# One loop for query mixing and the residual stage beside the edge products of a graph layer

## The chip, the cores and the metric

The kernel runs on one core of a Trainium2 chip. Times are device microseconds of that core for one execution. The time before is 3857.89 us, the median of 9 runs (3855.28 to 3866.76). The engines are named as the profile names them: PE (TensorE), DVE (VectorE), ACT (ScalarE), POOL (GpSimd) and SP (SyncE); SP only issues transfers here, and ACT and POOL issue some beside their own work.

## What is computed

A graph layer on 10,000 nodes with 512 features and 160,000 edges, sorted by destination, all in float32:

```python
xn = _layernorm(x, axis=-1)
x = x + _L0_gnn_ref(xn, W, bias, edge_weight, src, dst) + _L0_mix_ref(xn[None], w_qkv, w_out, gamma)[0]
x = x + _L0_ffn_ref(_layernorm(x)[None], router_w, W1, b1, W2, b2)[0]

# gnn: the kernel sums the rows of xn first and multiplies by W afterwards
h = X @ W;  msgs = h[edge_src] * edge_weight[:, None]
agg = segment_sum(msgs, edge_dst);  return relu(agg + bias)
# mix: linear attention, 8 heads of 64
q = softmax(q, axis=-1) * scale;  k = softmax(k, axis=-2)
context = einsum('bhnd,bhne->bhde', k, v)
out = einsum('bhde,bhnd->bhne', context, q);  out = gamma_layer_norm(out @ w_out.T, gamma)
# ffn: 6 experts, weights chosen from the mean row, gelu between W1 and W2
```

## The kernel before

The nodes are cut into 20 chunks of 512 rows (128 partitions by `SUB` = 4 rows; the last chunk has 272 rows). The stages follow each other, with the edge sums laid between the products of the first three:

- **Keys and queries.** `normal_rows` writes the normalised rows to DRAM (`xn_d`). For each chunk the loop computes the exponentials of keys and queries (`pk`, `pq`), adds keys times rows to `G`, and writes the transposed softmax of the queries to DRAM (`qT_d`).
- **Edges.** Edges are taken in groups of six tiles of 128. Line 327 gathers one tile of source rows by an indirect transfer that POOL issues (`msg`); lines 333 to 339 build on DVE a selection matrix `sel` (which of 64 destination rows a tile's edge belongs to, times its weight); line 345 multiplies them on PE (`pm`, two groups of three into the two halves of a PSUM bank); line 348 copies the sums out on ACT and line 349 writes them to `part_d` in DRAM. There are 209 groups, the last with two tiles. A destination whose edges cross a border between windows is put together by `carry`, for 128 windows (64 groups) at a time.
- **Mixing matrix.** After the keys, `edges_to(AT_HAND[0][1] // GROUP + 7)` runs edge groups with no other products between them until 135 are done; a conditional (`general_path`, line 456, not taken here) follows; then `mix` is computed (line 655 to 669), with one edge group between its steps.
- **Query loop.** For each chunk: load `qT` and the rows `xt` of x, multiply by `mix` (`po`, line 186), copy to `ot` on ACT, normalise (`row_stats`, lines 693 and 695, which also adds x), write to `y_d`.
- **Residual loop.** For each chunk: gather the edge sums by row (`at`, line 814, four indirect transfers), transpose them to `aT` (line 178, copied out by ACT and DVE in turn), multiply by the layer's weights (`pg`, line 186), add the bias (`gt`, line 836), apply relu and add `yt`, which is `y_d` loaded again (line 841), write `x1_d`, take the row statistics, normalise (`gt`, line 161), write `xn2_d`, and add the rows to `xsum` on POOL (line 849). `far_enough` runs edges up to the window that the chunk's rows may need (`AT_HAND`: chunks below 7 need windows below 256, chunks below 16 need 384, the rest all).
- **Experts.** 20 chunks of products with PE nearly always busy (line 1004). Their weights (`w1_sb`, `w2_sb`) are loaded when the edges are done and their memory is free (lines 741 and 742, from SP), and `w1_sum` is formed from them on DVE.

What sets the order: PE runs in the order of the program (`manual_schedule`). The other engines' streams are ordered by the framework's scheduler and then run in order. `work(us)` spreads the edges: each call counts the time of the products just issued (0.83 us per product of 128 by 512), and one group is issued for every `PACE` us counted. `msg` has 24 buffers, four groups. `row_stats` computes the inverse root on POOL (line 157, a power of -0.5), in one stream with the gathers. The products and transposes of the stages share six PSUM buffers, and the edge sums have two more.

Of the kernel before, what the change touches and what calls it, by code (L numbers as in the profile page):

```python
# [16 lines left out]
P = 128  # L17
SQ = 32
# [10 lines left out]
PACE = 5.4  # L29

AT_HAND = [(7, 256), (16, 384)]
# [8 lines left out]
def gps_layer_kernel(  # L40
# [41 lines left out]
    def tokens(t, c):  # L82
# [24 lines left out]
    from_last = const.tile([P, P], F32, name="from_last")  # L107
    nc.gpsimd.memset(from_last, 1.0)
    nc.gpsimd.affine_select(from_last, from_last, pattern=[[0, P]], compare_op=ALU.is_ge, fill=0.0,
                            base=1 - P, channel_multiplier=1)  # L110
# [21 lines left out]
    y_d = [dram.tile([r, SUB, D], F32, name=f"y_d{c}") for c, (_, r) in enumerate(chunks)]  # L132
# [8 lines left out]
    ZERO_ROW = NQ * P  # L141
    far_rows = -(-(N + P) // (8 * P)) * 8 * P
    assert far_rows <= AT_HAND[0][1] * WIN and NW < NQ * GROUP
    assert all(n <= NCH and w % P == 0 and w < NW for n, w in AT_HAND)
    part_d = dram.tile([ZERO_ROW + P, D], F32, name="part_d")
    by_window = part_d.rearrange("(w q) d -> w q d", q=WIN)
    nc.scalar.dma_start(part_d[ZERO_ROW : ZERO_ROW + P, :], zero)

    def row_stats(t, r, mv):

        st = small.tile([P, SUB, nc.vector.BN_STATS_DIM], F32, name="st")
        for s in range(SUB):
            nc.vector.bn_stats(st[:r, s, :], t[:r, s, :])  # L153
            nc.vector.bn_aggr(mv[:r, s, :], st[:r, s, :])
        ve = small.tile([P, SUB], F32, name="ve")
        nc.vector.tensor_scalar_add(ve[:r], mv[:r, :, 1], EPS)
        nc.gpsimd.tensor_tensor(mv[:r, :, 1], ve[:r], half_neg[:r], ALU.pow)
# [15 lines left out]
    def transposed(o, t, r, psum, tag):  # L173

        for kb in range(KB):
# [4 lines left out]
            (nc.scalar.copy if kb % 2 else nc.vector.tensor_copy)(  # L180
# [12 lines left out]

    edge_ctx = ctx.enter_context(ExitStack())
    query_ctx = ctx.enter_context(ExitStack())
    with ExitStack() as ph:
        mixing = edge_ctx.enter_context(tc.tile_pool(name="b_w", bufs=1))
        wq = mixing.tile([P, KB, D], F32, name="wq")
        G = mixing.tile([P, KB, D], F32, name="G")
# [16 lines left out]
        def normal_rows(n):  # L216

            for c in range(len(normal), min(len(normal) + n, NCH)):
# [4 lines left out]
                row_stats(xt, r, mv)  # L223
# [29 lines left out]
        def place_edges():  # L253
# [32 lines left out]
            nc.vector.memset(jump[:, 0:1], 1.0)  # L286
# [30 lines left out]
        def edges(i):  # L317
# [12 lines left out]
            sel = ew.tile([P, GROUP * BATCH, WIN], F32, name="sel")  # L330
# [8 lines left out]
            nc.vector.tensor_copy(sel[:, :n, 0:1], on_w[:, t0 : t0 + n, None])  # L339
            pm = psum_e.tile([P, D], F32, name="pm")  # L340
# [8 lines left out]
            nc.scalar.dma_start(part_d[i * P : (i + 1) * P, :], part)  # L349
# [3 lines left out]
        NJ = -(-NW // P)  # L353
        nexts = ep.tile([P, NJ], F32, name="nexts")
        held = {}
# [30 lines left out]
        def next_nodes():  # L386
            pn = psum.tile([P, NJ], F32, name="pnext", tag="ps")
            for b in range(NJ):
                r = min(P, NW - b * P)
                nc.tensor.transpose(pn[:r, b : b + 1], bases[0:1, b * P + 1 : b * P + 1 + r], ident[0:1, 0:1])  # L390
            nc.vector.tensor_copy(nexts[:, : NJ - 1], pn[:, : NJ - 1])
            r = NW - (NJ - 1) * P
            nc.vector.tensor_copy(nexts[:r, NJ - 1 :], pn[:r, NJ - 1 :])

        def carry_loads(b):
            r = min(P, NW - b * P)
            on = ew.tile([P, D], F32, name="on", bufs=1)
            nc.scalar.dma_start(on[:r], by_window[b * P : b * P + r, 0, :])
            own = ew.tile([P, D], F32, name="own", bufs=1)
            nc.scalar.dma_start(own[:r], by_window[b * P + 1 : b * P + 1 + r, 1, :])  # L400
            held["loads"] = on, own

        def carry(b):
            r = min(P, NW - b * P)
            on, own = held.pop("loads")
            to = bases[:, b * P + 1 : b * P + 1 + r]
# [3 lines left out]
            if b:  # L410
                same0 = ew.tile([P, P], F32, name="same0", bufs=1)
                nc.vector.scalar_tensor_tensor(same0[:, :r], to, bases[:, b * P : b * P + 1], from_last[:, :r],
                                               op0=ALU.is_equal, op1=ALU.mult)
            pt = psum.tile([P, D], F32, name="pcarry", tag="ps")
            nc.tensor.matmul(pt[:r], same[:r, :r], on[:r], start=True, stop=not b)
            if b:
                nc.tensor.matmul(pt[:r], same0[:, :r], held["total"], start=False, stop=True)
            if b < NJ - 1:
                held["total"] = ew.tile([P, D], F32, name="total", bufs=2)
                nc.scalar.copy(held["total"], pt)  # L420
            nc.vector.tensor_tensor(own[:r], own[:r], pt[:r], ALU.add)
            nc.scalar.dma_start(by_window[b * P + 1 : b * P + 1 + r, 1, :], own[:r])
# [4 lines left out]
        def edges_to(stop):  # L427
            while done[0] < stop:
                i = done[0]
                edges(i)  # L430
                done[0] += 1
                b, past_end = divmod(i, P // GROUP)
                if b and past_end == 1:
                    carry_loads(b - 1)
                if b and past_end == 6:
                    carry(b - 1)
# [197 lines left out]

        edges_to(AT_HAND[0][1] // GROUP + 7)
# [37 lines left out]
        dp = mean_ctx.enter_context(tc.tile_pool(name="d_w", bufs=1, side="right", reuse_waits="tile"))  # L673
        wg = dp.tile([P, KB, D], F32, name="wg")
        nc.sync.dma_start(wg, gnn_w.rearrange("(k p) d -> p k d", p=P))
        xsum = dp.tile([P, D], F32, name="xsum")
        nc.vector.memset(xsum, 0.0)
        io = query_ctx.enter_context(tc.tile_pool(name="c_io", bufs=2, side="right", reuse_waits="tile"))
        for c, (_, r) in enumerate(chunks):
            qT = io.tile([P, KB, SUB * P], F32, name="qT")  # L680
            nc.sync.dma_start(qT[:, :, : SUB * r], qT_d[c])
            xt = io.tile([P, SUB, D], F32, name="xt")
            nc.sync.dma_start(xt[:r], tokens(x, c))
            ot = io.tile([P, SUB, D], F32, name="ot")
            for s in range(SUB):
                po = psum.tile([P, D], F32, name="po", tag="ps")
                times(po, qT, s, r, mix)
                work(KB * PRODUCT)
                nc.scalar.copy(ot[:r, s, :], po[:r, :])
            mv = small.tile([P, SUB, 2], F32, name="mv")  # L690
# [6 lines left out]
            nc.sync.dma_start(y_d[c], ot[:r])  # L697
# [3 lines left out]

    PAIRS = NBASE // 2
    PLAIN = range(2 * PAIRS, NBASE)
    HALF = 2 * P
    KH, DH = KB // 2, D // 2
    assert KB % 2 == 0 and NF - NBASE <= PAIRS and all(fsz[f] == P for f in range(NBASE))
    def sums_of(o, a11, a12, a21, a22):

        nc.vector.tensor_tensor(o[0], a21, a22, ALU.add)
        nc.vector.tensor_tensor(o[2], a11, a21, ALU.subtract)
        nc.vector.tensor_tensor(o[1], o[0], a11, ALU.subtract)
        nc.vector.tensor_tensor(o[3], a12, o[1], ALU.subtract)

    def sums_for(o, b11, b12, b21, b22):

        nc.vector.tensor_tensor(o[0], b12, b11, ALU.subtract)
        nc.vector.tensor_tensor(o[2], b22, b12, ALU.subtract)
        nc.vector.tensor_tensor(o[1], b22, o[0], ALU.subtract)  # L720
        nc.vector.tensor_tensor(o[3], b21, o[1], ALU.subtract)

    io_f = {}
    held_w = {}

    def experts_weights():
        wp = held_w["pool"] = ctx.enter_context(tc.tile_pool(name="f_w", bufs=1, reuse_waits="tile"))
        w1_sb = held_w["w1"] = wp.tile([P, KB, NBASE * P], F32, name="w1_sb")
        w2_sb = held_w["w2"] = wp.tile([P, NBASE, D], F32, name="w2_sb")
        held_w["w1_sum"] = wp.tile([P, 4, KH, PAIRS * P], F32, name="w1_sum")  # L730
        b1_sb = held_w["b1"] = wp.tile([P, NF], F32, name="b1_sb")
# [480 lines left out]
```

## Time and profile before

| What | us |
|---|---|
| median of 9 runs | 3857.89 |
| the profiled execution's own time | 3863.09 |
| its span | 3861.4 |
| keys and queries, to the last product | 0 to 1303.45 |
| edges alone | 1303.45 to 1405.54 |
| no PE work, up to the mixing matrix | 1405.54 to 1425.60 |
| mixing matrix | 1425.60 to 1465.10 |
| wait for the first queries | 1465.10 to 1477.95 |
| query loop | 1477.95 to 1849.60 |
| residual loop | 1849.60 to 2480.42 |
| experts | 2480.42 to 3861.4 |

The borders are starts and ends of PE instructions in the timeline. A product of 128 by 512 in float32 is two instructions on PE and takes about 0.88 us of its time; an edge group is twelve instructions. The 40 slices of the page are 96.5 us each. "Idle before" a line is the time in which its engine did nothing just before it, and after the arrow stands what ended that time; "issue" means that nothing the profile shows ended it, which for in-order streams is often the instruction ahead in the queue.

### The profile page before, as it was taken

The numbers are of one execution on the slowest core, as the hardware profiler recorded it, in microseconds if no ns is written. First come the engines' busy times: TensorE is split into PE (matmuls) and PEld (weight loads), VectorE is DVE, ScalarE is ACT, GpSimd is POOL, SyncE is SP. The second block draws the span as 40 slices with busy tenths as digits, with TensorE's granted clock in tenths as the row PEclk, the third lists the DMA queues.
The fourth block names the chain that finished last, engine by engine and source line by source line (L and its number), as shares of the span: only waits on it lengthen the run. The fifth ranks groups of instructions, "written<-read, shape, count | busy, mean of one in ns | idle before, by whom it ended". The sixth has DMA issues, their size and how long they took to land.

```text
span 3861.4 us, 35880 instructions
## 1 busy us (share of the span) xinstructions
PE 3538.1 (92%) x12896; PEld 2028.2 (53%) x12896; DVE 1767.1 (46%) x3659; ACT 649.0 (17%) x1233; POOL 1586.7 (41%) x1565
## 2 busy tenths in 40 slices
PE   6999999999999748999675797899999999999998
PEld 3434343434343213333231243478888888888887
DVE  7843333333333214555352375764554545455452
ACT  4311111111111101111100000021111212111121
POOL 7656666666666662477687675400000000000000
PEclk9999999999999878999888898999999999999999
DMA  9667777777777766799787678612222112222210
GB/s 368 243 197 242 233 226 249 228 254 224 251 220 227 223 204 231 289 343 341 233 287 246 204 259 252 222 44 55 77 55 77 53 49 74 55 77 55 74 37 35
DMA packets 227061, 706.06 MB, mean 183 GB/s; under 512 B 36151, under 2 KB 76087, under 8 KB 195024
## 3 DMA queue, kind: packets, MB, share of 16 engines
q0 software_dynamic: 106720, 348.25, 29.1%
q1 hardware_dynamic: 72656, 194.76, 15.6%
q10 hardware_dynamic: 47492, 160.60, 10.8%
q8 instruction: 106, 1.74, 0.2%
q14 instruction: 87, 0.71, 0.1%
HBM read 504.22 MB, written 199.26 MB: 182 GB/s over the span
## 4 chain that ended last, share of the span: by engine, by line
PE 47%; DVE 5%; issue 5%; DMA 4%; POOL 1%; ACTq 0%; ACT 0%; SPq 0%; DVEq 0%; POOLq 0%
PE px L1004 13%; PE pz L1004 9%; PE py L1004 9%; PE po L186 7%; PE pm L345 3%; PE pg L186 3%; PE ph L1004 2%; DVE gt L161 1%; DMA msg<-xn_d,src_sb 1%; DMA z_d<-xt 1%; POOL msg L327 1%; DVE st L153 1%; DVE yt L841 1%; DMA xt<-x_d 1%; DVE gt L836 1%
## 5 line engine op out<-in xcount | busy, mean ns | idle before, releaser
L327 POOL DMA_INDIRECT msg<-xn_d,src_sb x1250 | 1230.6, 984 | 625.8 <-issue 303.8
L345 PE MATMUL pm<-msg,sel 128*64 128x512 f32 x2502 | 630.4, 629 | 105.0 <-issue 72.5
L345 PEld LDWEIGHTS pm<-msg,sel 128*64 128x64 f32 x2502 | 171.0, 142 | 539.0 <-issue 460.2
L186 PE MATMUL pg<-wg,aT 128*128 128x512 f32 (+1 forms) x640 | 297.6, 621 | 50.8 <-DVE gt L836 43.9
L186 PE MATMUL po<-G,qT 128*128 128x512 f32 (+1 forms) x640 | 285.8, 600 | 15.8 <-DMA qT<-qT_d 12.8
L613 PE MATMUL pc<-xn,ek 128*128 128x512 f32 (+1 forms) x640 | 287.8, 597 | 1.5 <-DVE G L616 1.1
L186 PE MATMUL pk<-wk,xnT 128*128 128x512 f32 (+1 forms) x640 | 287.9, 600 | 1.4 <-issue 1.1
L186 PE MATMUL pq<-wq,xnT 128*128 128x512 f32 (+1 forms) x640 | 287.1, 599 | 0.0
L333 DVE TENSOR_TENSOR sel<-iota_w,place 128x378 f32<-128x378 f32 (+1 forms) x209 | 123.4, 590 | 351.4 <-remote 165.7
L348 ACT COPY part<-pm 128x512 f32<-128x512 f32 x209 | 122.5, 586 | 854.0 <-PE pm L345 450.8
L186 PEld LDWEIGHTS pg<-wg,aT 128*128 128x128 f32 (+1 forms) x640 | 122.9, 197 | 213.3 <-issue 151.1
L1004 PE MATMUL px<-xnT,w_sb 128*128 128x256 f32 (+1 forms) x800 | 204.6, 378 | 15.9 <-DVE u L1039 15.9
L186 PEld LDWEIGHTS po<-G,qT 128*128 128x128 f32 (+1 forms) x640 | 118.1, 188 | 182.9 <-issue 182.9
L186 PEld LDWEIGHTS pk<-wk,xnT 128*128 128x128 f32 (+1 forms) x640 | 117.0, 188 | 168.6 <-issue 164.0
L186 PEld LDWEIGHTS pq<-wq,xnT 128*128 128x128 f32 (+1 forms) x640 | 116.6, 187 | 168.0 <-issue 166.3
L613 PEld LDWEIGHTS pc<-xn,ek 128*128 128x128 f32 (+1 forms) x640 | 116.9, 190 | 144.0 <-issue 137.5
L1004 PE MATMUL px<-w_sb,hh 128*128 128x256 f32 (+1 forms) x800 | 186.3, 380 | 0.0
L1004 PE MATMUL py<-xs,w_sum 128*128 128x256 f32 (+1 forms) x800 | 185.0, 374 | 0.0
L1004 PE MATMUL py<-w_sum,hh 128*128 128x256 f32 (+1 forms) x800 | 179.2, 379 | 0.0
L1004 PEld LDWEIGHTS px<-xnT,w_sb 128*128 128x128 f32 x800 | 150.5, 192 | 39.0 <-DVE u L1039 19.2
L1004 PEld LDWEIGHTS px<-w_sb,hh 128*128 128x128 f32 (+1 forms) x800 | 150.6, 188 | 22.9
L1004 PEld LDWEIGHTS py<-w_sum,hh 128*128 128x128 f32 (+1 forms) x800 | 150.0, 188 | 22.7
(254 smaller groups left out, 4433.4 us busy)
## 6 DMA issues: line engine op xcount, KB each, us to landing
part_d<-part ACTq DMA_DIRECT2D x209, 256.0 KB
msg<-xn_d,src_sb POOLq DMA_INDIRECT x1250
xn<-in_x SPq DMA_DIRECT2D x19, 1024.0 KB
xn_d<-xn ACTq DMA_DIRECT2D x19, 1024.0 KB
qT_d<-qT ACTq DMA_DIRECT2D x19, 1024.0 KB
qT<-qT_d SPq DMA_DIRECT2D x19, 1024.0 KB
xt<-in_x SPq DMA_DIRECT2D x19, 1024.0 KB
y_d<-ot SPq DMA_DIRECT2D x19, 1024.0 KB
```

The costliest lines, as they stand in the source:

```text
L153: nc.vector.bn_stats(st[:r, s, :], t[:r, s, :])
L161: (nc.vector if s < SUB - pool else nc.gpsimd).tensor_scalar(o[:r, s, :], t[:r, s, :], mv[:r, s, 0:1], mv[:r, s, 1:2], op0=ALU.subtract, o ...
L186: nc.tensor.matmul(po[:r, :], t[:, kb, s * r : (s + 1) * r], w[:, kb, :], start=kb == 0, stop=kb == KB - 1)
L327: nc.gpsimd.indirect_dma_start(out=m[k], out_offset=None, in_=xn_d, in_offset=bass.IndirectOffsetOnAxis(ap=src_sb[:, t0 + k : t0 + k + 1], ...
L333: nc.vector.tensor_tensor(sel[:, :n, 1:], iota_w[:, None, :].to_broadcast([P, n, WIN - 1]), place[:, t0 : t0 + n, None].to_broadcast([P, n ...
L345: nc.tensor.matmul(pm[h * WIN : (h + 1) * WIN, :], sel[:, k, :], m[k] if k < n else m[0], start=j == 0, stop=j == BATCH - 1 or k >= n - 1, ...
L348: nc.scalar.copy(part, pm)
L613: nc.tensor.matmul(pc, ek[:r, s, cb * P : (cb + 1) * P], xn[:r, s, :], start=s == 0, stop=s == SUB - 1)
L836: nc.vector.tensor_tensor(gt[:r, s, :], po[:r, :], bias_b[:r], ALU.add)
L841: nc.vector.scalar_tensor_tensor(yt[:r], gt[:r], 0.0, yt[:r], op0=ALU.max, op1=ALU.add)
L1004: nc.tensor.matmul(o, lhs[j], rhs[j], start=start and j == 0, stop=stop and j == n - 1, skip_group_check=True)
```

## The change

The query loop and the residual loop become one loop over the chunks. A chunk's mixed rows stay in SBUF (`ot`); `y_d` with its write and its read is gone. The rows gathered for the branch (`at`) are transposed before the last of the four query products, all four copied by ACT, and the layer's products `pg` follow the query products of the same chunk. `pg` plus bias goes into the chunk's `xt`, which the mixing part has finished with; later the normalised rows go there too. `qT` and `aT` have one buffer each.

- The stretch of edges alone after the keys is taken out; `PACE` goes from 5.4 to 5.0; the window limits become finer (`AT_HAND`, `CARRIES`: carries after 128, 256, 320, 384 windows and the rest), and `part_d` is moved behind a region of its own for the untaken path.
- Gathers and selections of a group are issued two groups ahead of its products (`edges_in`, `AHEAD`), with four buffers of `sel`.
- `row_stats` after the keys takes the root on ACT and a reciprocal and one correction step on DVE; the normalisation at the start keeps POOL's power.
- `xsum` is added on DVE; `x1_d` and `xn2_d` are written from SP, not ACT; the experts' weights are loaded from POOL's queue, not SP's.
- `w1_sum` and the first chunk for the experts are formed inside the loop (`c == NCH - 3`, `c == NCH - 2`).

In the order of instructions that the changed program has, 132 groups lie before the end of the keys (122 before), 5 in the mixing matrix as before, and the other 72 in the new loop, between the second chunk and the middle of the sixteenth.

```diff
-PACE = 5.4
-AT_HAND = [(7, 256), (16, 384)]
+PACE = 5.0
+AT_HAND = [(5, 128), (11, 256), (14, 320), (17, 384)]
+CARRIES = [0, 128, 256, 320, 384]
+AHEAD = 2
+LEAD = 5
...
-        nc.gpsimd.tensor_tensor(mv[:r, :, 1], ve[:r], half_neg[:r], ALU.pow)
+        if on_pool:
+            nc.gpsimd.tensor_tensor(mv[:r, :, 1], ve[:r], half_neg[:r], ALU.pow)
+            return
+        root = small.tile([P, SUB], F32, name="root")
+        nc.scalar.activation(root[:r], ve[:r], AF.Sqrt)
+        nc.vector.reciprocal(root[:r], root[:r])
+        near = small.tile([P, SUB], F32, name="near")
+        nc.vector.tensor_tensor(near[:r], root[:r], root[:r], ALU.mult)
+        nc.vector.scalar_tensor_tensor(near[:r], near[:r], -0.5, ve[:r], op0=ALU.mult, op1=ALU.mult)
+        nc.vector.scalar_tensor_tensor(mv[:r, :, 1], near[:r], 1.5, root[:r], op0=ALU.add, op1=ALU.mult)
...
-                nc.sync.dma_start(w1_sb[g * SQ : (g + 1) * SQ, j, :], features(w1)[j, g, :, : NBASE * P])
-        nc.sync.dma_start(w2_sb, w2[: NBASE * P, :].rearrange("(f p) d -> p f d", p=P))
+                nc.gpsimd.dma_start(w1_sb[g * SQ : (g + 1) * SQ, j, :], features(w1)[j, g, :, : NBASE * P])
+        nc.gpsimd.dma_start(w2_sb, w2[: NBASE * P, :].rearrange("(f p) d -> p f d", p=P))
...
-            sel = ew.tile([P, GROUP * BATCH, WIN], F32, name="sel")
+            sel = ew.tile([P, GROUP * BATCH, WIN], F32, name="sel", bufs=AHEAD + 2)
...
+            return n, m, sel
+        def edges_summed(i, n, m, sel):
             pm = psum_e.tile([P, D], F32, name="pm")
...
         def edges_to(stop):
             while done[0] < stop:
                 i = done[0]
-                edges(i)
+                while len(held["edges"]) <= AHEAD and i + len(held["edges"]) < NQ:
+                    held["edges"].append(edges_in(i + len(held["edges"])))
+                edges_summed(i, *held["edges"].pop(0))
                 done[0] += 1
...
-        edges_to(AT_HAND[0][1] // GROUP + 7)
         keys_ctx.close()
...
+        def queries_in(c):
+            qT = io.tile([P, KB, SUB * P], F32, name="qT", bufs=1)
+            nc.sync.dma_start(qT[:, :, : SUB * chunks[c][1]], qT_d[c])
+            return qT
...
         for c, (_, r) in enumerate(chunks):
-            qT = io.tile([P, KB, SUB * P], F32, name="qT")
-            nc.sync.dma_start(qT[:, :, : SUB * r], qT_d[c])
-            xt = io.tile([P, SUB, D], F32, name="xt")
-            nc.sync.dma_start(xt[:r], tokens(x, c))
+            xt = xt_next
             ot = io.tile([P, SUB, D], F32, name="ot")
             for s in range(SUB):
+                if s == SUB - 1:
+                    aT = io.tile([P, KB, SUB * P], F32, name="aT", bufs=1)
+                    transposed(aT, at, r, psum, "ps", by_act=range(KB))
+                    if c + 1 < NCH:
+                        at = gathered(c + 1)
                 po = psum.tile([P, D], F32, name="po", tag="ps")
                 times(po, qT, s, r, mix)
-                work(KB * PRODUCT)
+                put_out(KB * PRODUCT)
                 nc.scalar.copy(ot[:r, s, :], po[:r, :])
+            if c + 1 < NCH:
+                qT = queries_in(c + 1)
+                xt_next = rows_again(c + 1)
             mv = small.tile([P, SUB, 2], F32, name="mv")
             row_stats(ot, r, mv)
...
-            nc.sync.dma_start(y_d[c], ot[:r])
+            for s in range(SUB):
+                po = psum.tile([P, D], F32, name="pg", tag="ps")
+                times(po, aT, s, r, wg)
+                put_out(KB * PRODUCT)
+                nc.vector.tensor_tensor(xt[:r, s, :], po[:r, :], bias_b[:r], ALU.add)
+            nc.vector.scalar_tensor_tensor(ot[:r], xt[:r], 0.0, ot[:r], op0=ALU.max, op1=ALU.add)
+            nc.sync.dma_start(x1_d[c], ot[:r])
+            mv = stats2[:, c]
+            row_stats(ot, r, mv)
+            nt = xt if c < NCH - 1 else wg
+            normalize(nt, ot, r, mv)
+            nc.sync.dma_start(xn2_d[c], nt[:r])
+            if c < NCH - 1:
+                for s in range(SUB):
+                    nc.vector.tensor_tensor(xsum[:r], xsum[:r], xt[:r, s, :], ALU.add)
+            if c == NCH - 3:
+                sums_of_weights()
+            if c == NCH - 2:
+                io_f["in"] = ctx.enter_context(tc.tile_pool(name="f_in", bufs=1, reuse_waits="tile"))
+                turn = turned_in(0, rows_turned(0, rows_in(0)))
...
-        for c in range(NCH):
-            if c == NCH - 1:
-                io_f["in"] = ctx.enter_context(tc.tile_pool(name="f_in", bufs=1, reuse_waits="tile"))
-                turn = turned_in(0, rows_turned(0, rows_in(0)))
-            if c + 2 < NCH:
-                waiting.append(gathered(c + 2))
-            residual(c, *ready.pop(0), (lambda: turn_next(c + 1)) if c + 1 < NCH else (lambda: None))
```

## The prediction

> **What bounds the kernel now.** I read the page's slices first, to find where PE is not full, then the busy times by stage, then the timelines of PE, DVE and POOL at the holes.
>
> ```profile
> PE   6999999999999748999675797899999999999998
> POOL 7656666666666662477687675400000000000000
> DMA  9667777777777766799787678612222112222210
> ```
>
> PE is full in the keys (slices 2 to 13) and in the experts (from 26). The holes lie in slices 14, 15 and 20 to 25. By stage (columns: window, length, busy us of PE, PEld, DVE, ACT, POOL, granted clock, DMA share, GB/s):
>
> ```profile
> 1303.45:1405.54 102.09, 55.51 (x170) 15.31 (x168) 14.46 (x39) 7.03 (x12) 70.30 (x74) 0.72 0.74 227
> 1405.54:1425.60 20.06, 0.00 (x1) 0.00 (x0) 3.88 (x10) 1.76 (x3) 9.98 (x11) 0.61 0.64 198
> 1465.10:1477.95 12.85, 0.04 (x1) 0.03 (x1) 0.48 (x1) 0.59 (x1) 5.32 (x6) 0.61 0.98 363
> 1477.95:1849.60 371.65, 368.64 (x1012) 142.28 (x1012) 207.02 (x415) 63.72 (x110) 200.22 (x193) 1.00 0.83 301
> 1849.60:2480.42 630.82, 472.03 (x1420) 195.23 (x1419) 314.27 (x521) 45.04 (x80) 430.61 (x427) 0.88 0.76 251
> 2480.42:3861.40 1380.98, 1347.78 (x6129) 1143.09 (x6127) 670.52 (x1356) 244.01 (x572) 5.40 (x5) 0.99 0.19 59
> ```
>
> Edges alone keep PE half busy, and at 0.72 of its clock, so even the busy time is swollen. The query loop is full at clock 1.00. The residual loop leaves 159 us of 631 idle at a clock of 0.88. What ends the idle time there, on PE:
>
> ```profile
> 1425.60 3.67 PE L178 MATMUL pt<-ident,G 128*128 128x128 f32 x16 [20.06 <-ACTq L456]
> 1880.02 0.47 PE L178 MATMUL pt<-ident,at 128*128 128x128 f32 x1 [30.41 <-DMA at<-part_d,row_of]
> 2022.70 6.15 PE L186 MATMUL pg<-wg,aT 128*128 128x512 f32 x8 [7.09 <-DVE gt L836]
> 2110.27 4.12 PE L345 MATMUL pm<-msg,sel 128*64 128x512 f32 x12 [17.38 <-issue]
> ```
>
> A conditional, the first gathered sums, DVE's bias add that frees a PSUM buffer, and a burst of edges without products between. Why DVE is late, from DVE's and then POOL's timeline:
>
> ```profile
> 2036.80 0.55 DVE L333 TENSOR_TENSOR sel<-iota_w,place 128x378 f32<-128x378 f32 x1 [0.18 <-issue]
> 2049.29 1.91 DVE L161 TENSOR_SCALAR gt<-yt,stats 128x512 f32<-128x512 f32 x4 [11.94 <-issue]
> ```
>
> ```profile
> 2047.24 0.95 POOL L327 DMA_INDIRECT msg<-xn_d,src_sb  x1 [0.30 <-issue]
> 2048.21 1.05 POOL L157 TENSOR_TENSOR stats<-ve,half_neg 128x4 f32<-128x4 f32 x1
> ```
>
> DVE stands 11.94 us for a root of 1.05 us that is queued on POOL behind gathers. So three things cost time: bursts of edges that run at the gathers' pace, the root in POOL's queue, and the start of a second loop.
>
> **The change, part by part.** All sums are against the profiled execution (span 3861.4).
>
> *Prices.* Eight products take 7.06 us on the full PE (sixteen instructions of `po` in the query loop), four 3.53. Sixteen transposes take 1.75. An edge group takes 2.73 (the timeline has 2.79 with overlap). Conditions as in the query loop, where PE lost 2.7 us in 260 with edges between.
>
> *Keys.* PACE 5.0 puts 132 groups there, not 122: 10 x 2.73 = +27.3 us, so the last product ends at 1330.75. The gathers keep up: issue distance 1.25 us (0.95 + 0.30), 7.5 us a group, against about 8.7 us of PE per group.
>
> *Edges alone* (13 groups in 102.09 us) go; ten are the ones just paid, three move to the loop.
>
> *The conditional's hole*, 20.06 us: PE waited for ACT, whose copies and the carry of that burst ran to 1422. Without the burst ACT should be close behind PE; what remains is at least the 3 us that DVE shows between its last instruction and the branch, at most the old 20. I take 12, nearer the middle because POOL still has up to 18 gathers (22 us) queued ahead of the branch.
>
> *Mixing matrix* 39.50 and *the first query load* 12.85 (DMA at 0.98): unchanged.
>
> *The merged loop.* PE's work per chunk is 8 x 3.53 + 1.75 = 30.0 us, for 20 chunks 600 (rows of the short chunk cost the same in `po`). The edges: 71.5 groups (the last is half) x 2.73 = 195.2. Three carries of 2.0: 6. Together 801 us. Before, the same work stood in 371.65 + 630.82 = 1002.5. What stalls remain:
> - POOL loses the roots and `xsum` (20 x 1.05 and 76 x 1.36 us). Per chunk with edges (5.2 groups) it needs 31 gathers and 4 row gathers. With gathers at 1.016 + 0.30 us (mean in the query loop's edges) and row gathers at 1.155 + 0.30 (residual loop), the 13.75 chunks with edges need 565 + 80 = 645 us, against 413 + 195 = 608 of PE; four groups of lead (32 us) cover most of the 37. At the undisturbed 1.25 it is 536 + 69 = 605 and nothing is lost. So 0 to 37; I take 12, since four buffered groups stand nearly against the whole deficit.
> - DMA: 5 MB for the chunk's rows (qT, xt, at, x1, xn2; two fewer than before, `y_d` out and in) and 5.2 x 1.83 MB of edges, 14.8 MB in 44.2 us, 335 GB/s. Slices 17 and 18 moved 343 and 341 GB/s with PE full. Hidden, with little to spare.
> - DVE gets `xsum` (4 x 0.69) and about five small steps of 0.2 for each root. Per chunk: selections 5.2 x 1.37, statistics 8 x 0.85, small steps 2.0, lines 693 and 695 8 x 0.75, bias 4 x 0.68, relu 2.3, normalise 4 x 0.55 (its median), `xsum` 2.8: 31.9 of 44.2 us with edges, 24.8 of 30.0 without. It has room, and PE may run four products past the last PSUM buffer that DVE owes. Where this cover is gone, rival two has the price.
> - The root moves into ACT's stream: ACT waits for DVE's variance, and behind it stand the copies of the next chunk's `po` and of `pm`. ACT needs 8 x 0.59 + 5.2 x 0.59 = 7.8 us a chunk, and `po` and `pm` have buffers for some 7 us: taken as nothing. One more table load is 1.28 us (the two in the trace), on ACT alone.
> - Start: `at` and `qT` are ready late: 0 to the old 30.41, I take 5, since the first transposes now stand behind three query products (10.6 us) and the row gathers behind the queue of edges only.
> - Weights: the sixteen loads of `w1` kept SP's queue 34.83 us in this trace; on POOL they stand ahead of the row gathers of the next-but-one chunk, and DVE's sums wait for them in the third chunk from the end. No row shows a plain load on POOL: between 0 and 30 us, I take 8.
> - The additional carry and odd waits: 3.
>
> Together 28, so the loop takes 829 us.
>
> *Sum:* 1330.75 + 12 + 39.5 + 12.85 + 829.2 + 1381 (experts, untouched) = 3605 us of span, 256 below. The execution's own time lies 1.7 above its span, and the median 5.2 below that execution: forecast 3602.
>
> [...] The row: in the edges of the query loop, with DVE busy 56% of the time, the mean gather takes 1.016 us against a least 0.94. [...]
>
> **Rivals.**
> 1. *The gathers set the pace in the loop* (14%). For: 645 against 608 above, and in the two bursts groups followed each other at 7.8 to 9.8 us (2121.56, 2130.74, 2140.62, 2148.45, 2157.61), some 9. Against: there each selection waited for the products before it; now it is two groups ahead. Price: 71.5 x 9 + 80 = 724 instead of 608 + 12: +104, 3706.
> 2. *DVE's chain sets the chunk* (9%). For: it is 83% full in the six chunks without edges, with two trips to ACT and one wait for each. Against: PSUM slack. At 36 us instead of 30 there and 47 instead of 44.2 with edges: 36 + 39 = +75, 3677.
> 3. *The stalls come back under new names* (6%): half of the residual loop's 159 idle us stays, +80: 3682. This is the change not doing what it says.
> 4. *Slower: the single qT buffer* (5%). The next queries can only be loaded after the last query product, and the load has four products (14.1 us) and with edges 7 us more to land. The first one took 11.02 us at a DMA share of 0.98. If 1 MB behind the rows of x takes 35 us or more, 14 us x 19 = 266 us eat the gain; at 37 us the time is about 3890.
>
> **How the numbers follow.** Forecast case 66%: its own range is stalls 0 to 90 instead of 28, the conditional 5 to 20, the first load 0 to 13: 3555 to 3672. The range reaches up to rivals 1 to 3, 3555 to 3725; below and above it stand about 15%. A time within 0.2% (8 us) of before is about what a measurement of this kernel cannot tell from no change. All cases but the fourth and some mishap unnamed end far below: faster 0.92, same 0.01, slower 0.07.
>
> **What would show it.** Right: no hole of edges before the conditional; one loop of about 830 us with PE at 0.95 or more and clock near 1.00; no PE wait on a DVE add above 2 us; experts starting near 2224. Wrong: PE waits on `msg` transfers (rival 1), on `xt`<-`pg` or `aT` (2, 3), on `qT` (4), or PE below 0.9 in the keys.

## The result and the profile after

The changed kernel takes 22220.37 us (median of 10 runs, 22209.49 to 22235.92), beside 3860.86 us for the kernel before (31 runs): 5.756 times as long, with an interval of 5.751 to 5.761. The forecast was 3602, and its range ended at 3725.

First the slices of the page of the changed kernel (span 22215.2 us, 40 slices of 555 us each):

```profile
PE   9951111111111111111111111111111114889999
POOL 6631111111111111111111111111111111017100
PEclk9975555555555555555555555555555557999999
DMA  7752222222222222222222222222222221028421
```

For some thirty slices no engine is busy for more than two tenths, and TensorE's granted clock stands at half. By stage (columns: window, length, busy us of PE, PEld, DVE, ACT, POOL, granted clock, DMA share, GB/s):

```profile
0.00:1362.10 1362.10, 1312.18 (x4179) 529.68 (x4179) 557.93 (x1330) 285.29 (x456) 899.25 (x894) 0.99 0.77 250
1362.10:1410.60 48.50, 0.01 (x1) 0.03 (x1) 3.05 (x10) 0.00 (x0) 1.41 (x2) 0.52 1.01 383
1410.60:18615.50 17204.90, 3113.79 (x3750) 852.26 (x3750) 2820.29 (x12496) 0.00 (x0) 3213.09 (x2498) 0.50 0.21 38
18615.50:19887.30 1271.80, 1041.04 (x2881) 480.81 (x2881) 485.83 (x960) 169.80 (x399) 3.52 (x3) 0.95 0.09 32
19887.30:19931.70 44.40, 30.49 (x126) 14.76 (x125) 12.46 (x37) 6.99 (x13) 24.54 (x26) 0.81 0.71 236
19931.70:20840.30 908.60, 834.60 (x2470) 330.26 (x2469) 515.16 (x1138) 138.35 (x275) 516.55 (x547) 0.96 0.77 260
20840.30:22215.20 1374.90, 1348.10 (x6130) 1142.36 (x6128) 667.99 (x1355) 244.26 (x573) 0.00 (x0) 0.99 0.20 60
```

The keys, the merged loop (908.6 us) and the experts are all there, each within a tenth of its forecast size, and so is the mixing matrix. Between them lie three stages that the kernel before does not have (the second to the fourth row), 18525 us in all. The costliest groups of the page say what they are:

```profile
L612 PE MATMUL pm_far<-m_far,sel_far 128*128 128x512 f32 x2500 | 2556.1, 1126 | 4352.3 <-DMA m_far<-xn_d,cs 4351.7
L598 PE MATMUL pd<-ident,cd 128*128 128x128 f32 x1250 | 557.6, 446 | 9787.4 <-DVE cw L592 9042.1
L615 POOL DMA_INDIRECT part_d<-part_far,to_far x1250 | 1983.2, 1587 | 6988.5 <-DVE part_far L614 6988.5
L594 POOL DMA_INDIRECT m_far<-xn_d,cs x1250 | 1232.5, 986 | 7051.4 <-DVE off L607 7041.4
```

These tiles, `m_far`, `part_far`, `pd`, belong to `all_edges`, the body of the conditional `general_path`: the sums of all 160,000 edges a second time, one tile of 128 edges after another. The branch that the kernel before leaves out is taken. After it comes `with_maxima` (1271.80 us), keys and queries a second time; before it, 48.50 us in which the region of `part_d` for this path is filled with zeros (383 GB/s). One turn of the loop, from the timeline (columns: start, length, engine, line, what, idle before and what ended it):

```profile
9010.28 0.15 DVE L588 COPY cs<-src_sb 128x1 int32 x1 [6.72 <-PEq L586]
...
9011.20 0.99 POOL L594 DMA_INDIRECT m_far<-xn_d,cs  x1 [5.77 <-DVE off L607]
...
9014.75 2.04 PE L612 MATMUL pm_far<-m_far,sel_far 128*128 128x512 f32 x2 [3.54 <-DMA m_far<-xn_d,cs]
9016.83 0.69 DVE L614 COPY part_far<-pm_far 128x512 f32<-128x512 f32 x1 [4.47 <-PE pm_far L612]
9017.80 1.59 POOL L615 DMA_INDIRECT part_d<-part_far,to_far  x1 [5.61 <-DVE part_far L614]
9024.10 0.15 DVE L588 COPY cs<-src_sb 128x1 int32 x1 [6.58 <-PEq L586]
```

Apart from a few DVE steps beside the gather, nothing overlaps: 0.92 us of small steps, 0.99 for the gather's issue, 2.56 until it has landed and PE starts, 2.08 of product, 0.97 of copy and hand-over, 1.59 for the scatter's issue, and 4.71 from its end to the next turn. That is 13.8 us; the stage has 17204.9 / 1250 = 13.76 for each of its 1250 turns.

**Why the branch is taken.** `place_edges` counts, among other things, how often each entry of `AT_HAND` holds; the body runs when the sum falls short of `ALL_GOOD`:

```python
for i, (n, w) in enumerate(AT_HAND):
    nc.vector.tensor_scalar(count[:, 2 + i : 3 + i], bases[:, w : w + 1],
                            float(chunks[n][0] if n < NCH else N), None, op0=ALU.is_ge)
```

`bases[w]` is the node at which window w begins, so an entry (n, w) asks whether the windows below w hold every edge of the chunks below n, and this depends on the edges. Their destinations are sorted and much denser among the low nodes. The table has the first nodes worked out from the inputs that the reference draws:

| window w | its first node in these edges | n allowed | entry before | entry after |
|---|---|---|---|---|
| 128 | 944 | 1 | | 5: needs 2560 |
| 256 | 3767 | 7 | 7: needs 3584 | 11: needs 5632 |
| 320 | 5902 | 11 | | 14: needs 7168 |
| 384 | 8481 | 16 | 16: needs 8192 | 17: needs 8704 |

Both old entries hold, all four new ones fail.

One more fact is needed to read the runs. They fell on chips of two kinds: on some the kernel before takes 3860 to 3866 us (as in the profile of before), here called the slower kind, on others 3790, the faster kind. Each chip was visited once, so what the text calls a chip's kind could also be something that held only during that visit. Each ratio below is to the kernel before on the same chip. One execution of the kernel before on a chip of the faster kind took 5676 us, at a granted clock of 0.61, and is left out of the ratios. "Finer limits" is the kernel of experiment 4.

### The profile page after: what moved, and what is told of

Its sections match the earlier page's. It is cut to its first block, busy times and chain, and to the rows that moved or that the text cites. A ratio compares the mean times of both kernels' runs of the same rounds, so it can differ in the third digit from the quotient of the medians.

```text
span 22215.2 us, 157299 instructions
## 1 busy us (share of the span) xinstructions
PE 7680.2 (35%) x19531; PEld 3350.2 (15%) x19531; DVE 5062.7 (23%) x17324; ACT 844.7 (4%) x1715; POOL 4658.4 (21%) x3968
## 3 DMA queue, kind: packets, MB, share of 16 engines
q8 instruction: 127, 2.08, 0.0%
## 5 line engine op out<-in xcount | busy, mean ns | idle before, releaser
L612 PE MATMUL pm_far<-m_far,sel_far 128*128 128x512 f32 x2500 | 2556.1, 1126 | 4352.3 <-DMA m_far<-xn_d,cs 4351.7
L598 PE MATMUL pd<-ident,cd 128*128 128x128 f32 x1250 | 557.6, 446 | 9787.4 <-DVE cw L592 9042.1
L615 POOL DMA_INDIRECT part_d<-part_far,to_far x1250 | 1983.2, 1587 | 6988.5 <-DVE part_far L614 6988.5
L594 POOL DMA_INDIRECT m_far<-xn_d,cs x1250 | 1232.5, 986 | 7051.4 <-DVE off L607 7041.4
L614 DVE COPY part_far<-pm_far 128x512 f32<-128x512 f32 x1250 | 864.0, 691 | 5507.3 <-PE pm_far L612 5507.3
L612 PEld LDWEIGHTS pm_far<-m_far,sel_far 128*128 128x128 f32 x2500 | 625.2, 310 | 4682.8 <-issue 4682.8
L600 DVE TENSOR_SCALAR sel_far<-pd,cd,cw 128x128 f32<-128x128 f32 x1250 | 511.2, 409 | 559.6 <-PE pd L598 559.6
L603 DVE SCALAR_TENSOR_TENSOR before<-pd,cd,earlier 128x128 f32<-128x128 f32 x1250 | 426.3, 341 | 0.0
L655 PE MATMUL pc<-xn_m,ktok 128*128 128x512 f32 (+1 forms) x640 | 344.7, 688 | 62.6 <-DVE ktok L652 62.6
L200 PE MATMUL pg<-wq,aT 128*128 128x512 f32 (+1 forms) x640 | 302.3, 619 | 53.5 <-ACT aT L194 33.3
```

The source lines that it names most:

```text
L200: nc.tensor.matmul(po[:r, :], t[:, kb, s * r : (s + 1) * r], w[:, kb, :], start=kb == 0, stop=kb == KB - 1)
L594: nc.gpsimd.indirect_dma_start(out=m, out_offset=None, in_=xn_d, in_offset=bass.IndirectOffsetOnAxis(ap=cs, axis=0))
L598: nc.tensor.transpose(pd, cd.to_broadcast([P, P]), ident)
L600: nc.vector.tensor_scalar(sel, pd, cd, cw, op0=ALU.is_equal, op1=ALU.mult)
L603: nc.vector.scalar_tensor_tensor(before, pd, cd, earlier, op0=ALU.is_equal, op1=ALU.mult, accum_out=seen)
L612: nc.tensor.matmul(pm, sel, m, start=True, stop=True)
```

## The experiments

All kernels but those of experiment 2 and the repeated kernel before are the changed kernel with the edge sums written from the start of `part_d` again, as before, and with the edits shown.

**1. Limits that these edges meet.**

```diff
-AT_HAND = [(5, 128), (11, 256), (14, 320), (17, 384)]
+AT_HAND = [(1, 128), (7, 256), (11, 320), (16, 384)]   # e1
+AT_HAND = [(7, 256), (16, 384)]                        # e0
```

> The changed kernel with window limits that this input's destinations meet, (1, 128), (7, 256), (11, 320), (16, 384), and the edge sums at the front of part_d again (so the untaken path would damage rows of the carry; it is not run). Theory G, the limits (5, 128), (11, 256), (14, 320), (17, 384) fail on this input and the conditional runs its body of 18,500 us: without the body 1362 (keys) + 15 + 44 + 13 + a loop of 909 as in the changed kernel + 3, 5 and 17 edge groups run without products between (14 buffered or not, some 95 us) + 1375 = about 3810 us. Rival N, the branch is on for another reason (norms, the place of the sums): still about 22,200 us.

> The changed kernel with the old limits (7, 256), (16, 384) and the edge sums at the front of part_d. Theory G: no body, but 3 and 37 edge groups without products between; 34 of them at some 8.5 us instead of 2.73, +200 on e1_limits without its bursts: about 3910 us. Rival N: about 22,200 us.

Measured: e1 3767.41 us, ratio 0.975 (0.973 to 0.977); e0 3851.79 (one run, beside 3859.72). The 18.5 ms are gone with four numbers. But the gain is 2.5%, not 6.6%, and with the two old limits hardly any is left. Both are 40 to 60 us below what was expected without the body.

**2. The kernel before with one limit too high.**

```diff
-AT_HAND = [(7, 256), (16, 384)]
+AT_HAND = [(8, 256), (16, 384)]
```

> The kernel before with one number changed, (8, 256) for (7, 256): the first 8 chunks are 4096 rows, and window 256 starts at node 3767. Theory G: the body runs here too, 17,205 us for the edges one tile at a time and 1272 us for keys and queries again: 3861 + 18,480 = about 22,340 us. Rival N: 3860 us.

Measured: 22691.74 us (one run), with the same 1250 turns of the body on its page. The kernel before, with none of the other edits, becomes as slow from one digit. That settles the guard as the cause of the factor: taken away it goes, put in alone it comes.

**3. The changed kernel with its own limits, and the guard made true.**

```diff
-                float(chunks[n][0] if n < NCH else N), None, op0=ALU.is_ge)
+                0.0, None, op0=ALU.is_ge)
...
-            nc.vector.tensor_scalar(row_of[:, c], at, float(ZERO_ROW), None, op0=ALU.min)
+            last_row = min([w * WIN - 1 for n, w in AT_HAND if c < n] + [ZERO_ROW])
+            nc.vector.tensor_scalar(row_of[:, c], at, float(last_row), None, op0=ALU.min)
```

> The changed kernel with its own window limits (5, 11, 14, 17), but each limit compared with node 0, so that the branch is never taken, and with each chunk's row numbers cut off at its limit. Rows of nodes past the limit are read from a wrong place: the sums of these nodes are left out, all instructions stay. So this is what the change would take on edges for which its limits held. Forecast as on record: 3602 (keys' end 1331, loop 829). By what the changed kernel's trace already showed of the same loop (keys' end 1362, loop 909): 1362 + 15 + 44 + 909 + 1375 = 3705, so that guard and missed sizes are two separate errors. If the loop was slow in that trace only because it came after the slow branch: about 3640.

Measured: 3580.09 us, ratio 0.9445 (0.943 to 0.946), on a chip of the faster kind. Its stages (the columns are those of the table by stage above):

```profile
0.00:1330.70 1330.70, 1296.22 (x4172) 525.76 (x4172) 560.40 (x1329) 288.37 (x455) 892.09 (x892) 0.99 0.79 252
1330.70:1344.20 13.50, 8.49 (x38) 5.26 (x36) 3.30 (x8) 1.76 (x3) 5.92 (x7) 0.75 0.89 288
1344.20:1369.00 24.80, 21.88 (x99) 9.83 (x98) 10.21 (x30) 5.28 (x9) 19.01 (x20) 1.00 0.87 270
1369.00:2203.00 834.00, 818.85 (x2471) 329.86 (x2470) 516.31 (x1138) 138.50 (x275) 519.28 (x552) 0.99 0.83 285
2203.00:3580.80 1377.80, 1348.88 (x6129) 1143.60 (x6127) 668.63 (x1355) 244.46 (x573) 0.00 (x0) 0.99 0.20 59
```

Keys' end 1330.7 (forecast 1330.75), loop 834.0 (829), experts 1377.8 (1381). On this chip the sum of the forecast came out, and what it left out was the branch. That the total agrees within 1% is partly luck: its prices come from a chip of the slower kind, and as a ratio the gain is 5.55%, not 6.6%. This kernel reads some rows from a wrong place; the finer limits of experiment 4, which read the right ones, take 835.1 us for the loop on the same chip.

**4. Finer limits, all of them met.** The bursts of e1 come from coarse limits: an entry forces all groups below its window at once, 5 groups before chunk 7 and 17 before chunk 11. More entries spread them:

```diff
+AT_HAND = [(1, 128), (7, 256), (9, 288), (11, 320), (13, 352), (15, 368), (16, 384)]
+CARRIES = [0, 128, 256, 288, 320, 352, 368, 384]
-LEAD = 5
+LEAD = 2
```

> The kernel with limits that these edges meet, cut finer: (1,128), (7,256), (9,288), (11,320), (13,352), (15,368), (16,384), with a carry at each cut and two groups of lead; PACE 5.0. The bursts of 5 and 17 groups go. Theory P: the loop still runs at the gathers' pace where it has edges (68 groups x 8.7 us and 80 row gathers x 1.45 us), and takes about 905, as in the changed kernel's trace: 1368 + 49 + 905 + 1377 = 3699. Theory B (only the bursts cost time): the loop takes 829 to 845, so 3625 to 3640. Without effect: 3767.

Measured: 3584.06 us, ratio 0.9456 (0.944 to 0.947). Below e1's time and below the numbers of both theories; but on a chip of the other kind than e1's. So the next four ran on one chip.

**5. Which part is the chip's.** The kernel before, e1, the finer limits and PACE 4.4 (experiment 6) once more, on one chip.

> The kernel before, unchanged, for its profile on the same chip as the three that follow. The kernels with met limits and with PACE 4.4 ran on a chip where the kernel before takes 3860; those with finer limits ran on one where it takes 3790, and so far the two differ in kernel and chip at once. Theory C (the chip: on the slower one the gathers come less often): if this chip is of the slower kind, 3855 to 3866 with 102 us of edges alone at a clock near 0.72; if of the faster kind, 3785 to 3795, and the 70 us are missing in the stretches of edges alone and the residual loop, not in the experts, 1377 to 1381.

> The kernel with limits (1,128), (7,256), (11,320), (16,384) once more, beside the finer limits on one chip. Theory B (its bursts of 5 and 17 groups cost it the time against the finer limits): 30 to 80 us slower than those on this chip, whatever the chip is. Theory C (the difference was the chip's): within 25 us of those.

> The kernel with finer limits once more. On a chip of the faster kind 3584 as before (keys' end 1332, loop 835). On one of the slower kind Theory C gives what the changed kernel's trace showed of its keys and loop: 1365 + 49 + 905 + 1377 = 3696, 0.957 of the kernel before; if the chip matters only for kernels with bursts: keys' end 1332 and 3584 to 3610.

> The kernel with PACE 4.4 once more. On a chip of the slower kind the keys end at 1504 and the time is 3765. On one of the faster kind Theory C gives a keys' end between 1381 (PE's work alone, as with half the gathers) and 1430, and a time of 3610 to 3680; if the keys end near 1500 there too, the gathers' pace is the kernel's own and not the chip's.

Measured, on a chip of the faster kind: before 3788.43; e1's kernel 3639.5, ratio 0.9606 (0.958 to 0.963); finer limits 3582.6, ratio 0.9455 (0.944 to 0.947); PACE 4.4 3599.45 (one run, 10 us below the range expected). So both theories hold, each for a part: the bursts cost 57 us on one chip, and the same kernel of e1 has the ratio 0.975 on one kind of chip and 0.961 on the other. Where the kinds differ shows in the kernel before. Its edges alone, 102.09 us in the profile of before, take 81.11 here, and the pause after them 6.27 instead of 20.06 (same columns):

```profile
1301.21:1382.32 81.11, 64.54 (x170) 15.96 (x168) 16.41 (x44) 8.19 (x14) 61.92 (x64) 0.98 0.82 253
1382.32:1388.59 6.27, 0.00 (x1) 0.03 (x1) 1.10 (x3) 0.58 (x1) 4.75 (x6) 0.83 0.89 271
```

PE is busy for 0.80 of the stretch instead of 0.54, at a clock of 0.98 instead of 0.72. The query and residual loops together take 970.5 us instead of 1002.5. The experts, with no gathers, take the same on both (1381.9 here, 1380.98 there).

A third time, the kernel with finer limits fell on the other kind:

> The kernel with finer limits a third time, for its place beside the three kernels that undo one part of it, which ran where the kernel before takes 3866. On such a chip, by Theory C as written down before: 3696 or 0.957. If the undone parts are worth what Theory R and Theory S say, it must lie 40 or more below 3703 and 3712, at 3660 or less (0.947); by Theory N it lies within 10 us of them, 3693 to 3713. On a chip of the faster kind: 3583 again.

Measured: 3700.18 us, ratio 0.9588 (0.957 to 0.960), within 5 us of Theory C's 3696. The loop of this run by the windows view (columns as above):

```profile
1405.70:2307.50 901.80, 843.87 (x2483) 333.41 (x2482) 516.10 (x1147) 139.75 (x278) 522.47 (x547) 0.96 0.77 262
```

and the loop of the same kernel on the faster kind, e10:

```profile
1369.10:2202.30 833.20, 819.03 (x2484) 328.33 (x2483) 517.86 (x1147) 139.72 (x278) 523.47 (x552) 0.99 0.83 285
```

The same instructions, 69 us apart: 44 of it PE idle (58 against 14), 25 more of PE busy, at a granted clock of 0.96 instead of 0.99. What ended PE's waits from the mixing matrix to the end of the loop (engine, tile, line, what it waited for, total us, times, longest), first e16 on the slower kind:

```profile
PE pg L200 <- issue: 19.2, 16, 2.8
PE pm L461 <- issue: 15.2, 12, 2.1
...
PE pg L200 <- ACT aT L194: 11.7, 1, 11.7
```

and e10 on the faster kind, in its loop:

```profile
PE pt L192 <- DMA at<-part_d,row_of: 7.0, 4, 4.4
PE pm L461 <- DMA msg<-xn_d,src_sb: 4.6, 6, 1.1
PE po L200 <- DMA qT<-qT_d: 2.3, 1, 2.3
```

On the faster kind every wait has a transfer's name and they are small. On the slower kind most are "issue", for which the profile shows no cause.

**6. The gathers' pace in the keys.**

```diff
-PACE = 5.0
+PACE = 4.4   # e3, e5, e11: limits of e1
+PACE = 4.7   # e12: finer limits
...
# e5 only, in edges_in
-                    if k < n:
+                    if k < n and h and j < n - BATCH:
+                        m[k] = m[j]
+                    elif k < n:
```

> As e1_limits, with PACE 4.4: 150 edge groups before the end of the keys, and no group runs without products between. Theory G with the loop limited by PE: keys 1362 + 18 x 2.73 = 1411, 15 + 44 + 13, loop 909 - 49 = 860, 1375: about 3720 us. If the gathers cannot keep up with 4.4 in the keys (7.5 us a group against 46.3 / 8.9 + 2.73 = 7.9): keys up to 1450 and 3760 us. Rival N: about 22,200 us.

> The kernel with PACE 4.4, but each group gathers three tiles of messages instead of six and uses each for both windows: half the messages are left out, PE's products, selections and sums stay. Theory P (the gathers' pace on POOL, some 1.45 us each, is what the keys ran at with PACE 4.4): the keys end at 1303 + 28 x 2.78 = 1381 instead of 1504 and PE stays full, and the loop loses its bursts, so about 3600. Theory D (PE itself, DVE's selections or ACT's copies set the pace): keys' end within 20 us of 1504 and the time within 30 us of 3765.

> The kernel with finer limits and PACE 4.7, so that some eight groups move from the loop to the keys. Theory P: the loop is still held a little by the gathers (moving ten groups into it cost 60 there and gave 29 back in the keys), so 8 x 2.8 = 22 us more keys and 25 to 45 us less loop: 0 to 20 us faster than with finer limits at PACE 5.0, 3565 to 3584 on a chip of the faster kind (kernel before 3790). If PE's work alone counts: the same within 5 us.

Measured: e3 3764.69 us, ratio 0.9756 (0.973 to 0.978), keys' end 1503.9, beyond the 1450 expected, on the slower kind. e5 3544.46 (one run), keys' end 1384.7, on the faster kind; but there e11, with all its gathers, also ends its keys at 1385.1, so halving them changes nothing in the keys and e5 does not decide between P and D for the slower kind, where neither was run with half the gathers. What e3 and e11 show is one kernel on the two kinds. POOL's gathers between 400 and 1300 us by the groups view (busy time, mean ns, then the idle time before them), first e3:

```profile
L439 POOL DMA_INDIRECT msg<-xn_d,src_sb x622 | 607.3, 976 | 293.8 <-issue 147.3 <-remote 56.2 <-PE pm L461 49.5
```

and e11:

```profile
L439 POOL DMA_INDIRECT msg<-xn_d,src_sb x686 | 666.0, 971 | 233.8 <-issue 136.5 <-PE pm L461 55.9 <-DMA msg<-xn_d,src_sb 25.5
```

One gather in 900 / 622 = 1.447 us against 1.312: 8.7 us a group against 7.9. A gather's issue is as long on both (976 and 971 ns); the time between them differs. On the slower kind the number of gathers in this window hardly moves with the pace asked for: 621 at PACE 5.0 (e1), 615 at 4.7 (e12), 622 at 4.4 (e3). On the faster kind it goes from 635 (e10) to 686, and PE is busy for all 900 us in both.

e12, on the slower kind: 3745.51, ratio 0.9693 (0.967 to 0.972), keys' end 1440.5. That is 1.05% of the kernel before, 40 us, slower than the finer limits at PACE 5.0 on such a chip (0.9588), where 0 to 20 faster was expected for a chip of the faster kind: eight groups more in the keys cost 65 us there, beside two kernels on the same chip with the same keys at PACE 5.0 (e13 and e15, keys' end 1374.3 and 1375.9), some 8 each instead of 2.8.

In the loop the halved gathers do count. The loops of e5 and then e11:

```profile
1419.40:2168.10 748.70, 746.25 (x2255) 311.55 (x2254) 492.05 (x1084) 127.97 (x257) 244.97 (x276) 1.00 0.62 213
1421.90:2219.40 797.50, 773.42 (x2255) 319.42 (x2254) 493.65 (x1084) 128.74 (x257) 411.33 (x445) 0.99 0.75 257
```

The same instructions on PE, 49 us apart on two chips of the faster kind. At PACE 4.4 so many groups are done before the loop that neither has a burst in it, so the gathers cost time there without one.

**7. Ten groups from the keys to the loop.**

```diff
-            edges_to(min(NQ, int(done[1] / PACE)))
+            edges_to(min(NQ, int(done[1] / pace[0])))   # 5.4 in the keys, 4.8 in the loop
```

> As the kernel with finer limits, but with PACE 5.4 in the keys (122 groups) and 4.8 in the loop, so that ten groups move from the keys to the loop. The keys should end near 1310 instead of 1368. Theory P: in the loop each of the ten costs a full 8.7 us of gathers, +87 there, so 20 to 35 us slower than with finer limits alone, about 3725. Theory B: 2.8 us each there, so some 30 us faster, about 3600 to 3670.

Measured: 3613.93 us, ratio 0.9531 (0.951 to 0.955), on the chip of e4, e5 and e6: 30 us slower than the finer limits, Theory P's side. The keys end at 1303.1, 28.6 earlier (2.86 a group); the loop takes 895.2, 60.1 more (6.0 a group). PE's longest wait in that loop is for gathers, 16.2 us in all.

**8. Three parts of the change undone, one by one, on the finer limits.**

```diff
-            row_stats(ot, r, mv)
+            row_stats(ot, r, mv, on_pool=True)     # e13, e17: both roots of the loop
-AHEAD = 2
+AHEAD = 0                                          # e14
-                    transposed(aT, at, r, psum, "ps", by_act=range(KB))
+                    transposed(aT, at, r, psum, "ps")   # e15
```

> The kernel with finer limits, with the two roots of each chunk of the loop back on POOL (the part of the change that took them off undone). Theory R (a root behind gathers holds DVE, and DVE holds PE's PSUM buffers: 11.94 us of DVE idle for one root before): about 14 chunks with edges x 2 roots x 2 to 5 us of PE = 50 to 140 us slower than with finer limits. Theory N (the buffers and the selections made ahead hide it): within 10 us.

> The kernel with finer limits, with no group ahead: selections and gathers of a group are put out just before its products, as in the kernel before. Theory S (selections late on DVE and gathers late on POOL are what made the edges stall): the loop at some 8.5 us a group as in the bursts before, 68 x (8.5 - 8.3) plus the stall of each chunk's DVE work, 40 to 100 us slower. Theory N (the four groups of message buffers are lead enough): within 10 us of the finer limits.

> The kernel with finer limits, with the copies of the transposed gathered sums shared between ACT and DVE as before, not all on ACT. In the changed kernel's trace PE waited 33.3 us for these copies. If ACT is what was late: 10 to 30 us faster. If that wait only took over what the gathers would have cost anyway: within 6 us on a chip of the faster kind, where no such wait is left.

> The kernel with finer limits and the roots back on POOL, beside the finer limits on one chip. Theory R: 50 us or more slower than those; Theory N: within 10 us.

All on chips of the slower kind, e16 and e17 on the same one:

| kernel | us | ratio to before, interval |
|---|---|---|
| finer limits (e16) | 3700.18 | 0.9588 (0.9572 to 0.9604) |
| roots on POOL (e13) | 3702.77 | 0.9573 (0.9549 to 0.9598) |
| roots on POOL (e17) | 3685.43 | 0.9548 (0.9532 to 0.9564) |
| nothing ahead (e14) | 3712.24 | 0.9596 (0.9569 to 0.9623) |
| copies shared (e15) | 3702.64 | 0.9584 (0.9563 to 0.9606) |

None of the three, undone alone, makes the kernel measurably slower. With the roots back on POOL it is 15 us faster beside e16 on one chip (e17), with intervals just apart, and by the ratio 6 us on another chip (e13). So Theory R and Theory S fall for the changed kernel on the slower kind; no run undoes two parts together, and none on the faster kind.

## Why the prediction was wrong

**The step that failed** is the conditional's. The prediction priced "the conditional's hole" as a wait, "at least the 3 us that DVE shows", "at most the old 20", and took 12. It never asked whether the conditional would still not be taken, though the change rewrites the numbers that its guard compares with the data. In place of the 12 us stood 18525. Sorted random destinations can be spread in many ways; the limits (5, 128), (11, 256), (14, 320), (17, 384) would hold for even ones (128 of 417 windows begin at about node 3070 of 10,000) and fail for these. No row of the profile of before could show it, as there is no instruction of the branch in it; the guard's code and the edges could. The rival on the slower side, the single `qT` buffer, was not it: PE waits 2.3 to 5.4 us in all for `qT` in the loops of e4, e6, e10 and e16. The slower end lay in "some mishap unnamed", which names no mechanism.

**The other terms**, against the finer limits on the kind of chip that the forecast was made for (e16), on the faster kind (e10), and in the changed kernel's trace:

| term | forecast | e16 | e10 | changed kernel |
|---|---|---|---|---|
| keys' end, 132 groups | 1330.75 | 1350.5 | 1331.0 | 1362.1 |
| conditional, mixing matrix, first load | 64.35 | 55.2 | 38.1 | 44.4 (mixing matrix alone) |
| merged loop | 829.2 | 901.8 | 833.2 | 908.6 |
| experts | 1381 | 1378.8 | 1375.8 | 1374.9 |
| span | 3605 | 3686.3 | 3578.1 | 22215.2 |

- *Keys.* "The gathers keep up, 7.5 us a group against about 8.7" held on the faster kind to the microsecond. On the slower kind it was mis-sized: 7.5 is the issue distance of an undisturbed run of gathers, while over 900 us of keys they came 1.45 us apart at each of three paces, 8.7 us a group, so the margin was nil. The keys end 20 to 49 us late in the runs at PACE 5.0 with 132 groups. That the gathers are what held PE there is argued from their number: PE's waits are "issue", and no run on this kind has half the gathers.
- *Conditional, mixing matrix, first load.* Mis-sized the other way. In e10 PE works for 7.9 of the 13.4 us between the keys and the mixing matrix, the mixing matrix takes 24.7 us at clock 1.00, not 39.50, and the wait for the first load is 2.3, not 12.85. Part of this is the chip's: the kernel before takes 6.27, 32.56 and 13.13 us for the three there (e8).
- *Merged loop.* PE's work was put at 801 and stalls at 28. On the faster kind 819 and 14: right in sum. On the slower kind 844 and 58. The forecast's price of PE's instructions came from the query loop, at clock 1.00; in e16's loop the clock is 0.96 and the same instructions take longer.
- *Roots and selections.* The reason given for DVE's lateness, a root behind gathers on POOL, described the trace before but was not what a root costs: in the merged loop, roots on POOL cost no time (e13, e17). Shown is what bursts cost, 57 us for those of e1; that the stalls went because edges now lie beside twice the products is argued.
- *The weights' loads on POOL*, bounded at 0 to 30 us of PE's time and taken as 8, show as 16 issues of 0.50 us, 8 us of POOL's time. That the figures are the same is chance: none of PE's waits in e10's loop, 13.9 us in all, names them.
- *Gathers beside `xsum`.* With `xsum` on DVE in the loop, 0.68 us an addition, the mean gather issue is 1.037 us (e10), against the 1.016 of the query loop before.
- *Rivals.* The gathers as the loop's pace (rival 1): in part, and on both kinds. On the faster one ten groups more in the loop cost 60 us (experiment 7) and half the gathers save 49 at PACE 4.4 (experiment 6). On the slower one the loop takes 902, between the 829 of the forecast and the 933 of the rival, but PE's waits there do not name gathers. The stalls under new names (rival 3): of its 80 us, 58 idle on the slower kind, 14 on the faster. The DVE chain (rival 2) and `qT` (rival 4): neither. (Rival 4's "about 3890" at 37 us is 3904 by its own numbers.)

What would have shown it, "one loop of about 830 us with PE at 0.95 or more" and "no edge hole before the conditional", is seen in e4, e6 and e10 (PE 819 of 833 us). Had the limits held, then by these stand-ins the forecast would have been 1.2% low for the faster kind's ratio (0.9445 against 3602 / 3857.89 = 0.934), and the slower kind's 3700 would lie in the range given, above the likeliest case's own 3672.

**What stays open**: why one kind of chip spaces the same gathers wider, and what lies behind "issue" there. On the faster kind PE never waited between 400 and 1300 us of the keys, even at 1.312 us a gather (e11), so no limit of the gathers was reached there.

## What to carry to other kernels

A constant that a guard compares with the data is part of the algorithm: before the cost of a change is summed, evaluate each such guard on the actual input, since a profile without the branch can't price it, and a body of dependent steps can cost far more than the whole kernel. A margin between two engines' paces should be taken from a long stretch in which both work, not from the shortest distance of an undisturbed run, and on more than one chip. A reason read from one wait ("DVE stands 12 us for a root") is a hypothesis on the chain, not on the time: undoing that part alone in the changed kernel showed it to be worth nothing there.

## What was not expected of the hardware

The same kernel differed by 118 us between chips (finer limits: 3582.6 and 3700.18); of the 108 us between the two profiles, 105 lie ahead of the experts, in the stages with gathers. A stage of dependent steps with PE busy for 18% of the time ran at a granted clock of 0.50. A loop with one gather, one transpose, one product and one scatter-add in each turn took 13.76 us a turn, 4.71 of it between the end of the scatter's issue and the next turn.
